# A decoder layer with a mixture of experts: scatters free of one another, another order of score products, more first blocks and more places for blocks

## The chip, the cores and the metric

The kernel runs on one core of one Trainium2 chip. Its five engines appear in the profile as PE (matrix products into PSUM; its weight loads are PEld), DVE (vector work), ACT (activations and copies), POOL (vector work, and here the issue of indirect DMAs, called scatters) and SP (issue of all other DMAs). The metric is device time in microseconds of one execution, lower is better.

## The reference

One decoder layer on 32 sequences of 128 tokens with 128 features: causal self-attention with 16 heads of 8, cross-attention with a second input, and a mixture of 8 experts of which each token uses two; a residual and a layer norm behind each. All in float32.

```python
x = _layernorm(x + _attn(x, x, x, sa_wq, ..., True), ln1_g, ln1_b)
x = _layernorm(x + _attn(x, encoder_output, encoder_output, ca_wq, ..., False), ln2_g, ln2_b)
x = _layernorm(x + _moe(x, router_w, router_b, e_w1, e_b1, e_w2, e_b2), ln3_g, ln3_b)

def _moe(x, rw, rb, w1, b1, w2, b2):
    router_weights = softmax(xf @ rw + rb)
    topw, topi = top_k(router_weights, 2); topw = softmax(topw)
    h = gelu(einsum('td,edf->etf', xf, w1) + b1)        # 128 -> 512
    eo = einsum('etf,efd->etd', h, w2) + b2              # 512 -> 128
    out = sum over the two experts of topw * eo
```

## The kernel before

**The plan.** The kernel states its work as tasks: an engine, an estimated duration, a priority, the tasks it depends on and the buffers it uses. `Plan.run` is a list scheduler. It plays the tasks through with the estimates and the constants `LINK`, `SWITCH`, `PE_LAT` and `CLOCK` at the top of the file, hands out places from pools (`Slots` for SBUF, `Banks` for PSUM), and thereby fixes one order of instructions for each engine. `Plan.emit` writes the instructions in that order and adds what each must wait for: the last instruction of each task it depends on, and the earlier users of its places. For pairs of other engines' instructions it declares that no dependency is to be found by the tensors' addresses (`declare_no_dep`), except on what is kept; for instructions of the same engine it does not. A DMA issued by POOL belongs to POOL's own queue group, so two scatters into one DRAM tensor remain dependent on each other, each on the one ahead.

**Attention.** The 32 sequences are 8 groups of 4 (`NG`, `G`). `prepare` loads a group's input by SP, transposes it on PE (L725), and projects it to q, k (L732, L735) and v (L778). `emit_step` (L835) writes the score products of 59 steps of two halves each. A half computes scores with queries on partitions for the row maxima, taken by DVE (L922), and, three steps later, scores with keys on partitions, to which the negated maxima are added by a product (`sel`) before ACT takes the exponential (L1320); there are 112 halves of each, 14 to a group. All products go through the helper `mm`, L833, which is also used for the products with V. Between the two stands the path of the maxima: POOL splits them into two bfloat16 parts (L934, L935, tile `nmx`), PE transposes them (L942, `nmT`), ACT or DVE copies them out. Norms run on DVE (L1050, L1051) with a power and an affine step on POOL (L1056, L1057, L1147, L1148).

**Routing and rows.** After the cross-attention of a group, `finish_cross` (L1129) computes router scores (L1155), ranks the tokens of each expert with counts on DVE, POOL (L1194 to L1199) and PE (L1206, L1207), and scatters each token's normalised row twice, once per expert, into the DRAM tensor `rows_d`: eight scatters of 128 rows a group (L1227), 64 in all. Eight fill scatters (L1521) complete the last block of each expert.

**Blocks.** `block` (L1544) is called for `NS` = 71 blocks of 128 rows of one expert. SP loads the rows (L1554) and the expert's w1 (L1577, 256 KB); PE transposes the rows (L1565), ACT scales them (L1570), PE does four products with w1 (L1583), ACT four gelus (L1592), PE four products with w2 (L1600), DVE adds b2 (L1610, L1613) and POOL scatters the result into `res_d` (L1618). The first `NF` = 17 blocks use the rows of groups 0 to `GF` = 3 only; the others wait for all rows and the fills. The transposes of all blocks wait for the last attention step (`last_step`). Places are: two of `s_in` for even and four of `s_xT` for odd rows, two of `s_q` for their transposes, three for w1, four for results (`s_o`); a block's PSUM banks come from the four that `kept` leaves to single banks.

**The last norm.** `final` (L1625) loads a group's results (L1632, 512 KB), weights and adds them (L1643, L1646), norms and stores (L1660). It waits for the scatters of a number of blocks, and its tasks stand in the engines' orders between the blocks.

## Time and profile before

| | us |
|---|---|
| median of 3 runs (lowest, highest) | 921.33 (912.32, 924.99) |
| the profiled execution | 923.84 |
| its span, first to last instruction | 922.1 |
| PE, PEld busy | 641.8, 518.2 |
| DVE, ACT, POOL busy | 343.0, 323.2, 259.4 |
| mean granted PE clock | 0.832 |

The views used below: the page gives busy time and the chain of work that ended last, followed backwards; the view of a tile or a line lists its instructions with their durations, and what its engine waited for ahead of them; the waits of an engine sum idle time by what ended it; a timeline lists instructions by start; windows sum busy time in a stretch, with the granted PE clock (1.00 is full) and the DMA engines' mean share and rate. "A <- B" in an instruction reads "A is written from B".

### The profile page before, as it was taken

The numbers are of one execution on the slowest core, as the hardware profiler recorded it, in microseconds if no ns is written. First come the engines' busy times: TensorE is split into PE (matmuls) and PEld (weight loads), VectorE is DVE, ScalarE is ACT, GpSimd is POOL, SyncE is SP. The second block draws the span as 40 slices with busy tenths as digits, with TensorE's granted clock in tenths as the row PEclk, the third lists the DMA queues.
The fourth block names the chain that finished last, engine by engine and source line by source line (L and its number), as shares of the span: only waits on it lengthen the run. The fifth ranks groups of instructions, "written<-read, shape, count | busy, mean of one in ns | idle before, by whom it ended". The sixth has DMA issues, their size and how long they took to land.

```text
span 922.1 us, 31269 instructions
## 1 busy us (share of the span) xinstructions
PE 641.8 (70%) x12884; PEld 518.2 (56%) x12884; DVE 343.0 (37%) x1009; ACT 323.2 (35%) x717; POOL 259.4 (28%) x440
## 2 busy tenths in 40 slices
PE   1888889895986896878957775460776466667760
PEld 1666667673765674657845544450666456567650
DVE  3644445552553453546643514210111431321231
ACT  1233453521632523525313322230244254534430
POOL 4000100213322213231132223423332353423442
PEclk9989999988897997999976857595689798977775
DMA  6200100001001001000002001130344354444321
GB/s 171 83 16 15 38 26 15 27 15 36 26 29 34 14 21 42 19 22 15 5 25 65 17 10 41 44 98 29 84 121 110 112 147 118 127 124 136 105 61 46
DMA packets 53012, 52.73 MB, mean 57 GB/s; under 512 B 7759, under 2 KB 39415, under 8 KB 52872
## 3 DMA queue, kind: packets, MB, share of 16 engines
q1 hardware_dynamic: 44976, 40.74, 15.1%
q0 software_dynamic: 4576, 9.00, 3.0%
q8 instruction: 103, 1.69, 0.8%
q10 hardware_dynamic: 3320, 1.00, 0.5%
q14 instruction: 37, 0.30, 0.1%
HBM read 35.36 MB, written 11.61 MB: 51 GB/s over the span
## 4 chain that ended last, share of the span: by engine, by line
PE 38%; issue 20%; DMA 18%; POOL 10%; DVE 7%; ACT 3%; ACTq 1%; SPq 1%; POOLq 1%; DVEq 0%
PE ps L833 23%; DMA res_d<-o,id 11%; POOL rows_d L1227 6%; DMA rows_d<-y,rid 3%; PE ps L1583 3%; PE ps L1600 2%; DMA pr<-res_d 2%; DVE nm L922 2%; ACT pr L1320 2%; PE ps L778 1%; PE ps L735 1%; PE ps L732 1%; PE ps L1123 1%; PE ps L1155 1%; PE ps L725 1%
## 5 line engine op out<-in xcount | busy, mean ns | idle before, releaser
L922 DVE TENSOR_REDUCE nm<-ps 128x8 f32<-128x1024 f32 (+1 forms) x112 | 136.9, 1224 | 160.5 <-PE ps L833 147.9
L1320 ACT ACTIVATE pr<-ps 128x1024 f32<-128x1024 f32 x112 | 114.7, 1024 | 195.4 <-PE ps L833 182.2
L833 PE MATMUL ps<-k,qm 32*64 32x128 f32 (+1 forms) x4096 | 174.6, 279 | 6.0 <-issue 3.7
L833 PEld LDWEIGHTS ps<-k,qm 32*64 32x64 f32 x4096 | 134.0, 139 | 32.2 <-issue 29.9
L833 PE MATMUL ps<-qm,k 32*64 32x512 f32 (+1 forms) x1024 | 136.6, 609 | 17.5 <-ACT pr L1320 7.0
L1592 ACT ACTIVATE k<-ps,b1c 128x128 f32<-128x128 f32 x284 | 81.1, 372 | 117.6 <-PE ps L1583 75.1
L1583 PE MATMUL ps<-q,w 128*128 128x128 f32 x568 | 97.3, 328 | 33.4 <-DMA w<-in_L_xattn_e_w_dram 22.7
L1618 POOL DMA_INDIRECT res_d<-o,id x71 | 69.9, 985 | 154.0 <-DMA res_d<-o,id 117.2
L1600 PE MATMUL ps<-wall,k 128*128 x568 | 97.1, 325 | 18.4 <-ACT k L1592 11.8
L1583 PEld LDWEIGHTS ps<-q,w 128*128 128x128 f32 x568 | 88.2, 237 | 37.8 <-issue 16.6
L1600 PEld LDWEIGHTS ps<-wall,k 128*128 128x128 f32 x568 | 86.1, 232 | 25.9 <-ACT k L1592 17.8
L1227 POOL DMA_INDIRECT rows_d<-y,rid x64 | 63.8, 997 | 122.5 <-DMA rows_d<-y,rid 109.3
L833 PE MATMUL ps<-pr,v 64*32 64x128 f32 (+2 forms) x3072 | 77.9, 274 | 9.5 <-issue 6.3
L833 PEld LDWEIGHTS ps<-pr,v 64*32 64x32 f32 (+1 forms) x3072 | 60.1, 114 | 22.3 <-issue 12.1
L934 POOL CAST nmx<-nm 128x16 bf16<-128x16 f32 x64 | 12.8, 200 | 198.5 <-DVE nm L922 196.9
L1570 ACT ACTIVATE q<-ps,col_b,col_g 128x128 f32<-128x128 f32 x71 | 33.1, 470 | 75.9 <-PE ps L1565 75.3
L833 PEld LDWEIGHTS ps<-qm,k 32*64 32x64 f32 x1024 | 33.3, 139 | 36.9 <-ACT pr L1320 20.5
L833 PE MATMUL ps<-nmT,sel 32*64 32x128 bf16 x1792 | 51.7, 229 | 2.8 <-issue 2.8
L1610 DVE TENSOR_SCALAR id<-xin,tab_e 128x1 int32<-128x1 f32 x36 | 9.8, 273 | 114.7 <-PE ps L1600 59.0
L942 PE MATMUL ps<-ident,nmx 128*128 128x128 bf16 x64 | 13.4, 240 | 51.4 <-POOL nmx L935 50.2
L833 PEld LDWEIGHTS <-sel 32*64 32x64 bf16 x1792 | 38.2, 111 | 13.2 <-issue 11.8
L1565 PE MATMUL ps<-ident,xT 128*128 128x128 f32 x35 | 11.7, 336 | 45.5 <-DVE o L1613 30.7
(261 smaller groups left out, 857.4 us busy)
## 6 DMA issues: line engine op xcount, KB each, us to landing
w<-in_L_xattn_e_w_dram SPq DMA_DIRECT2D x71, 256.0 KB
qm<-q SPq DMA_DIRECT2D x64, 64.0 KB
pr<-res_d SPq DMA_DIRECT2D x8, 512.0 KB
xin<-rows_d SPq DMA_DIRECT2D x36, 65.0 KB
xT<-rows_d SPq DMA_DIRECT2D x35, 65.0 KB
xin<-in_x_dram SPq DMA_DIRECT2D x8, 256.0 KB
xin<-in_ctx_dram SPq DMA_DIRECT2D x8, 256.0 KB
wall<-in_L_xattn_e_w_dram SPq DMA_DIRECT2D x8, 256.0 KB
```

Source lines behind the costliest of these rows:

```text
L833: nc.tensor.matmul(out_, lhsT=lhsT, rhs=rhs, start=start, stop=stop, skip_group_check=True)
L922: lambda: nc.vector.tensor_reduce(dst(), src(), AX.X, ALU.max, negate=True), [dep], [pair, nm],
L934: nc.gpsimd.tensor_copy(nmx.at[:, a, :, 0:4], src[:, a])
L942: nc.tensor.transpose(b16[:, a * P : (a + 1) * P], nmx.at[:, a].rearrange("p g c -> p (g c)"), ident16)
L1227: nc.gpsimd.indirect_dma_start(out=rows_d[:, :], out_offset=bass.IndirectOffsetOnAxis(ap=rid.at[:, i, k : k + 1], axis=0), in_=y.at[:, i, ...
L1320: lambda kp=kp, prb=prb, kh=kh: nc.scalar.activation(prb.at[:, 8 * kh : 8 * kh + 8, :].rearrange("p h q -> p (h q)"), kp.at.rearrange("p b ...
L1565: nc.tensor.transpose(bt.at[:, 0:P], xr_()[:, 0:P], ident)
L1570: lambda: nc.scalar.activation(xT.at[:, 0:P], bt.at[:, 0:P], AF.Identity, bias=cols["b2"], scale=cols["g2"]),
L1583: nc.tensor.matmul(p1.at[:, c * P : (c + 1) * P], lhsT=w1.at[:, c, :], rhs=xT.at[:, 0:P], start=True, stop=True)
L1592: nc.scalar.activation(h.at[:, c, :], p1.at[:, c * P : (c + 1) * P], AF.Gelu, bias=b1c[:, bass.ds(r + c, 1)],)
L1600: nc.tensor.matmul(p2.at[:, 0:P], lhsT=h.at[:, c, :], rhs=flat[:, bass.ds(w["pe"] + c * P, P)], start=c == 0, stop=c == NFC - 1,)
L1618: nc.gpsimd.indirect_dma_start(out=res_d[:, :], out_offset=bass.IndirectOffsetOnAxis(ap=idb.at[:, 0:1], axis=0), in_=o.at, in_offset=None, ...
```

## The change

- **Scatters.** In `emit`, a task on POOL whose instruction is a DMA is now also declared free of POOL's earlier DMAs, except of those its task or its places name. The eight scatters of a group name none of each other.
- **Order of score products.** `emit_step` collects its pieces (scores with n, masks, `sel` products) with the work time of their row group up to them, and sorts both halves' pieces by it. Cross-attention steps come out as before.
- **Transposes in order.** The transposed input of self-attention is no longer kept as halves interleaved by sequence pair. A projection is one product of 512 columns instead of two of 256; V of self-attention is eight products with 64 rows of result instead of four; the residual in `wo` is one product a sequence instead of two halves.
- **Blocks.** 25 first blocks (`NF`) from groups 0 to 4 (`GF` = 4); blocks take any of eight PSUM banks; rows take any of the six places (`Either`); the transposed rows have three places of their own (`s_bx`); w1 of blocks from 25 on goes into twelve places in the tiles of `qm` (`s_late`).
- **Planner.** `LINK`, `PE_LAT`, `CLOCK` and many durations have new values.

```diff
-LINK = 0.12
+LINK = 0.07
-PE_LAT = 0.1
-CLOCK = 1.08
+PE_LAT = 0.06
+CLOCK = 1.0
...
+class Either(Slots):
+    def take(self, n):
+        for s in self.kinds:
+            if s.free:
+                return s.take(n)
+        return None
...
-        order = [i for i in range(len(self.tiles) - 1, self.kept - 1, -1)]
+        order = list(range(len(self.tiles) - 1, (self.kept if n == 1 else 0) - 1, -1))
...
-                    if key[0] != i.engine:
+                    if key[0] != i.engine or (key[1] and line(i)[1] and t.eng == "POOL"):
                         tc.declare_no_dep(i, group=name, keep=kept, reason="apart, by the plan")
...
-    NF = 17
-    GF = 3
+    NF = 25
+    GF = 4
...
+    s_bx = Slots(places(3, [P, P], "bx"))
...
-        for a in range(2):
-            nc.tensor.matmul(
-                bank[:, 2 * P * a : 2 * P * (a + 1)], lhsT=w,
-                rhs=xT.rearrange("p (a h) (k t) -> p a k h t", a=2, k=2)[:, a], start=True, stop=True,
-            )
+        nc.tensor.matmul(bank, lhsT=w, rhs=xT.rearrange("p s t -> p (s t)"), start=True, stop=True)
...
+                for k in range(2):
+                    nc.tensor.matmul(
+                        bv.at[HALF * k : HALF * k + HALF, i * P : (i + 1) * P],
+                        lhsT=xT.at[:, i - i % 2 + k, HALF * (i % 2) : HALF * (i % 2) + HALF], rhs=raw["wvs"],
+                        start=True, stop=True, skip_group_check=True,
+                    )
...
+            for n in range(len(cols_[0])):
+                nq = cols_[0][n][3]
+                work.append((at, lambda n=n: scores_k(n)))
+                at += 16 * nq * PASS
...
+        for _, fn in sorted(work, key=lambda w: w[0]):
+            fn()
...
-                    for h in range(2):
-                        mm(by.at[HALF * h : HALF * h + HALF, s * P : (s + 1) * P], xs[:, s // 2, s % 2, h], ident, False, False)
+                    nc.tensor.matmul(o, lhsT=it.xT.at[:, s, :], rhs=ident, start=False, stop=False)
...
+    s_xr = Either(s_in, s_xT)
+    s_late = Slots([q_[:, r].rearrange("p (c f) -> p c f", c=NFC) for q_ in qm_t for r in range(4)])
...
-        xr = Buf((s_in, s_xT)[s % 2])
+        xr = Buf(s_xr)
...
-        bt, xT = Buf(s_ps), Buf(s_q)
+        bt, xT = Buf(s_ps, 0), Buf(s_bx)
...
-        p1, p2, h, w1 = Buf(s_ps), Buf(s_ps), Buf(s_k), Buf(s_w1)
+        p1, p2, h, w1 = Buf(s_ps, 0), Buf(s_ps, 0), Buf(s_k), Buf(s_w1 if s < NF else s_late)
```

The line numbers of the kernel after the change are about 40 higher: L1227 becomes L1266, L1618 becomes L1659, L1577 becomes L1618, L934 and L935 become L975 and L976. A name in brackets behind "waits" is a semaphore: that of an engine, or of one of the eight lanes that POOL's DMAs (DMASW) and SP's (DMAHW) take in turn.

The first place is POOL around the scatters of group 0, before:

```order
L934 CAST nmx_164<-nm_161 128x4x4 [waits DVE_49]
L935 TENSOR_TENSOR nmx_164<-nm_161,nmx_164 128x4x4 [waits Pool_49]
L1227 DMA rows_d<-y_185,rid_203 33920x130 [waits DVE_49,Activation_49,DMAHW1_49]
L1227 DMA rows_d<-y_185,rid_203 33920x130 [waits DMASW0_49]
L1227 DMA rows_d<-y_185,rid_203 33920x130 [waits DMASW1_49]
L1227 DMA rows_d<-y_185,rid_203 33920x130 [waits DMASW2_49]
L1227 DMA rows_d<-y_185,rid_203 33920x130 [waits DMASW3_49]
L1227 DMA rows_d<-y_185,rid_203 33920x130 [waits DMASW4_49]
L1227 DMA rows_d<-y_185,rid_203 33920x130 [waits DMASW5_49]
L1227 DMA rows_d<-y_185,rid_203 33920x130 [waits DMASW6_49]
L1056 TENSOR_SCALAR rs_195<-mv_191 128x4 [waits DVE_49]
```

and of the change:

```order
L975 CAST nmx_166<-nm_163 128x4x4 [waits DVE_49]
L976 TENSOR_TENSOR nmx_166<-nm_163,nmx_166 128x4x4 [waits Pool_49]
L1266 DMA rows_d<-y_188,rid_206 33920x130 [waits DVE_49,Activation_49,DMAHW2_49]
L1266 DMA rows_d<-y_188,rid_206 33920x130 x7
L1097 TENSOR_SCALAR rs_198<-mv_194 128x4 [waits DVE_49]
L1098 TENSOR_TENSOR rs_198<-rs_198,mhalf 128x4 [waits Pool_49]
L975 CAST nmx_167<-nm_164 128x4x4 [waits DVE_49]
L976 TENSOR_TENSOR nmx_167<-nm_164,nmx_167 128x4x4 [waits Pool_49]
L1183 COPY y_188<-tok_84 128x4 [waits DMASW4_49,DMASW5_49,DMASW3_49,DMASW6_49,DMASW2_49,DMASW7_49,DMASW1_49,DMASW0_49]
```

Before, each scatter from the second on waits for the lane of the one ahead of it; now the seven behind the first wait for nothing, and the first instruction that waits for all lanes is the reuse of the tile that they read.

The second place is POOL at the end of attention, where group 7's scatters, the fills and the first scatters of block results (to `res_d`) stand, before:

```order
L1618 DMA res_d<-o_256,id_263 8192x128 [waits DVE_49]
L1227 DMA rows_d<-y_186,rid_204 33920x130 [waits DMASW3_49,DMASW2_49,DMASW4_49,DMASW1_49,DMASW5_49,DMASW0_49,DMASW6_49,DVE_49,DMASW7_49,PE_49,Activation_49]
L1227 DMA rows_d<-y_186,rid_204 33920x130 [waits DMASW1_49]
L1227 DMA rows_d<-y_186,rid_204 33920x130 [waits DMASW2_49]
L1227 DMA rows_d<-y_186,rid_204 33920x130 [waits DMASW3_49]
L1227 DMA rows_d<-y_186,rid_204 33920x130 [waits DMASW4_49]
L1227 DMA rows_d<-y_186,rid_204 33920x130 [waits DMASW5_49]
L1227 DMA rows_d<-y_186,rid_204 33920x130 [waits DMASW6_49]
L1227 DMA rows_d<-y_186,rid_204 33920x130 [waits DMASW7_49,DMASW0_49]
L1521 DMA rows_d<-fillrow,fid 33920x130 [waits DVE_49,DMASW0_49]
L1521 DMA rows_d<-fillrow,fid 33920x130 [waits DMASW1_49]
```

and of the change, from the last scatter of group 7 on:

```order
L1266 DMA rows_d<-y_189,rid_207 33920x130 [waits DMASW7_49]
L1560 DMA rows_d<-fillrow,fid 33920x130 [waits DVE_49,DMASW0_49]
L1560 DMA rows_d<-fillrow,fid 33920x130 [waits DMASW1_49]
L1560 DMA rows_d<-fillrow,fid 33920x130 [waits DMASW2_49]
L1560 DMA rows_d<-fillrow,fid 33920x130 [waits DMASW3_49]
L1560 DMA rows_d<-fillrow,fid 33920x130 [waits DMASW4_49]
L1560 DMA rows_d<-fillrow,fid 33920x130 [waits DMASW5_49]
L1560 DMA rows_d<-fillrow,fid 33920x130 [waits DMASW6_49]
L1560 DMA rows_d<-fillrow,fid 33920x130 [waits DMASW7_49]
L1659 DMA res_d<-o_259,id_266 8192x128 [waits DMASW0_49]
L1659 DMA res_d<-o_260,id_267 8192x128 [waits DVE_49,DMASW1_49]
L1659 DMA res_d<-o_261,id_268 8192x128 [waits DVE_49,DMASW2_49]
```

Before, one result's scatter stands ahead of group 7's rows, and each waits for the lane ahead. Now all of group 7's scatters and the fills stand ahead of the first result's, and each waits for its own lane, which is the eighth scatter before it.

The third place is SP at the loads of w1 (into `w`, and now into tiles of `qm`) and of rows (`xin`, `xT`), before:

```order
L1540 TENSOR_LOAD tab_x [waits DMAHW0_49,PE_49]
L1577 ISA
L1577 DMA w_261<-in_L_xattn_e_w_dram 128x512 [waits DMAHW0_49,PE_49]
L1540 TENSOR_LOAD tab_x [waits DMAHW1_49,PE_49]
L1577 ISA
L1577 DMA w_262<-in_L_xattn_e_w_dram 128x512 [waits DMAHW1_49,PE_49]
L1540 TENSOR_LOAD tab_r [waits DMAHW3_49,DVE_49]
L1554 ISA
L1554 DMA xin_137<-rows_d 128x130 [waits DMAHW3_49,DVE_49]
```

and of the change:

```order
L1581 TENSOR_LOAD tab_x [waits DMAHW2_49,PE_49]
L1618 ISA
L1618 DMA w_263<-in_L_xattn_e_w_dram 128x512 [waits DMAHW2_49,PE_49]
L1581 TENSOR_LOAD tab_x [waits DMAHW3_49,PE_49]
L1618 ISA
L1618 DMA w_264<-in_L_xattn_e_w_dram 128x512 [waits DMAHW3_49,PE_49]
L1581 TENSOR_LOAD tab_x [waits DVE_49]
L1618 ISA
L1618 DMA qm_152<-in_L_xattn_e_w_dram 128x512
L1581 TENSOR_LOAD tab_x
L1618 ISA
L1618 DMA qm_152<-in_L_xattn_e_w_dram 128x512 [waits DMAHW4_49]
```

Before, a load of w1 waits for PE to be done with one of the three places; now two in a row do so, and those behind them go to the places in `qm` and wait for no engine.

## Rows read from the trace of the kernel before

**Rows 1.** The page, part 1: busy time, share of span, instructions of each engine.
```profile
PE 641.8 (70%) x12884; PEld 518.2 (56%) x12884; DVE 343.0 (37%) x1009; ACT 323.2 (35%) x717; POOL 259.4 (28%) x440
```

**Rows 2.** The page, part 4: shares of the chain that ended last.
```profile
PE 38%; issue 20%; DMA 18%; POOL 10%; DVE 7%; ACT 3%; ACTq 1%; SPq 1%; POOLq 1%; DVEq 0%
```

**Rows 3.** View of tile rows_d: engine idle before its instructions until (us, times).
```profile
  DMA rows_d<-y,rid: 112.0, 57
```

**Rows 4.** View of tile res_d: duration ns min/median/max, starts; idle before; landing.
```profile
L1618 POOL DMA_INDIRECT res_d<-o,id x71: 967/969/1098, 592.5 to 901.5; - x71
...
  DMA res_d<-o,id: 117.2, 48
...
DMA to landing us min/median/max: 2.1/2.4/5.3
```

**Rows 5.** Timeline of POOL, 204 to 233 us: start, duration, line, operation, [idle before].
```profile
206.99 1.44 POOL L1227 DMA_INDIRECT rows_d<-y,rid  x1 [1.25 <-DVE rc L1020]
...
228.71 0.97 POOL L1227 DMA_INDIRECT rows_d<-y,rid  x1 [1.62 <-DMA rows_d<-y,rid]
...
231.07 0.20 POOL L934 CAST nmx<-nm 128x16 bf16<-128x16 f32 x1
```

**Rows 6.** Waits of PE, 204 to 552 us: us in total, times, longest.
```profile
PE ps L942 <- POOL nmx L935: 50.2, 8, 10.7
```

**Rows 7.** Windows of attention: length, PE PEld DVE ACT POOL busy, PEclk, DMA, GB/s.
```profile
204.00:550.00 346.00, 268.00 (x6797) 203.06 (x6785) 159.13 (x418) 120.28 (x198) 96.73 (x190) 0.85 0.08 25
289.00:337.00 48.00, 43.69 (x1323) 34.43 (x1312) 25.71 (x60) 22.80 (x37) 7.73 (x24) 0.93 0.08 25
```

**Rows 8.** The same windows, exponentials of L1320 alone: length, ACT busy (count).
```profile
204.00:550.00 346.00, 73.76 (x72) 0.85 0.08 25
289.00:337.00 48.00, 13.31 (x13) 0.93 0.08 25
```

**Rows 9.** Timeline 549 to 551 us: the last exponential.
```profile
550.24 1.02 ACT L1320 ACTIVATE pr<-ps 128x1024 f32<-128x1024 f32 x1 [0.76 <-PE ps L833]
```

**Rows 10.** View of line 1613, the block results on DVE: ns, first and last start.
```profile
L1613 DVE TENSOR_TENSOR o<-ps,b2r x71: 280/285/292, 585.1 to 898.2; 128x128 f32<-128x128 f32 x71
```

**Rows 11.** Windows of the blocks, columns as in rows 7.
```profile
620.00:640.00 20.00, 0.00 (x0) 0.00 (x0) 0.00 (x0) 0.00 (x0) 7.71 (x8) 0.56 0.07 24
670.00:680.00 10.00, 8.67 (x67) 7.89 (x67) 1.48 (x6) 5.00 (x17) 2.90 (x3) 1.00 0.46 140
720.00:730.00 10.00, 1.58 (x7) 1.61 (x8) 4.07 (x13) 0.00 (x0) 1.94 (x2) 0.58 0.65 211
```

**Rows 12.** Timeline of PE, 672 to 679 us.
```profile
673.09 1.12 PE L1583 MATMUL ps<-q,w 128*128 128x128 f32 x8
...
674.15 1.06 PE L1600 MATMUL ps<-wall,k 128*128 x8
675.04 1.06 PE L1583 MATMUL ps<-q,w 128*128 128x128 f32 x8
```

**Rows 13.** Waits of PE, 585 to 898 us.
```profile
PE ps L1565 <- DVE o L1613: 41.1, 14, 24.6
PE ps L1583 <- DMA w<-in_L_xattn_e_w_dram: 22.7, 8, 9.1
```

**Rows 14.** Timeline of POOL, 581 to 596 us.
```profile
592.50 1.02 POOL L1618 DMA_INDIRECT res_d<-o,id  x1 [0.55 <-issue]
594.14 0.97 POOL L1227 DMA_INDIRECT rows_d<-y,rid  x1 [0.62 <-DVE fid L1514]
```

**Rows 15.** Timeline of DVE, 206 to 209 us.
```profile
206.90 0.42 DVE L1028 TENSOR_TENSOR u<-u,rc 128x256 f32<-128x256 f32 x1
```

**Rows 16.** Timeline of SP, 498 to 506 us.
```profile
501.14 0.33 SPq L1554 DMA_DIRECT2D xin<-rows_d  x1
501.96 0.33 SPq L1577 DMA_DIRECT2D w<-in_L_xattn_e_w_dram  x1
```

**Rows 17.** Timeline of POOL, 894 to 923 us: the last scatter.
```profile
901.54 0.99 POOL L1618 DMA_INDIRECT res_d<-o,id  x1 [2.17 <-DMA res_d<-o,id]
```

More of the change, by code (lines that the diff above doesn't have):

```diff
@@ L63, with __init__ @@
 class Place:
-    def __init__(self, ap):
-        self.ap, self.last = ap, []
+    def __init__(self, ap, home=None):
+        self.ap, self.last, self.home = ap, [], home
 class Slots:
     def __init__(self, aps):
-        self.free = [Place(ap) for ap in aps]
+        self.free = [Place(ap, self) for ap in aps]
     def take(self, n):
@@ L80, in take, with give, __init__ @@
         return p.ap, [p]
-    def give(self, places):
-        self.free += places
+    def give(self, places, front=False):
+        for p in places:
+            p.home.free.insert(0 if front else len(p.home.free), p)
+class Either(Slots):
+    def __init__(self, *kinds):
+        self.kinds = kinds
+    def take(self, n):
[3 more added lines that the diff above has]
+        return None
 class Banks:
@@ L108, in take, with give @@
         return None
-    def give(self, places):
+    def give(self, places, front=False):
         for i, hs in enumerate(self.halves):
@@ L195, in run @@
                         for b in reversed(taken):
-                            b.slots.give(b.places)
-                            if isinstance(b.slots, Slots):
-                                b.slots.free.insert(0, b.slots.free.pop())
+                            b.slots.give(b.places, True)
                             b.at, b.places = None, []
@@ L713, with transposes @@
     before = {}
-    def transposes(src, prio, deps, bufs, halves=False):
+    def transposes(src, prio, deps, bufs):
         bank = Buf(s_ps)
@@ L751, in prepare @@
         xT = it.xT = Buf(s_xT)
[L752 removed]
+        bank, t = transposes(lambda: it.xin.at, t0 - 6, [ld], [it.xin, xT])
         it.t_tr = t
@@ L837, in emit_step, with rows @@
         kh = 1 - h
+        work = []
+        PASS = 0.427e-3
+        def rows(half, i):
+            rg = 2 * half + i
+            return slice(32 * rg, 32 * rg + 32)
         if sk is not None:
@@ L840, in emit_step, with scores_k @@
             cols_ = sk_cols(sk)
-            for n in range(len(cols_[0])):
+            at = 0.0
+            def scores_k(n):
                 for i in range(2):
-                    rg = 2 * kh + i
-                    rr = slice(32 * rg, 32 * rg + 32)
+                    rr = rows(kh, i)
                     for ct in range(2):
@@ L896, in emit_step, with top_k @@
+            def top_k(r):
+                for i in range(2):
+                    rr = rows(kh, i)
                     for ct in range(2):
@@ L1051, in stats @@
                 nc.vector.bn_aggr(mv.at[:, i, :], st.at[:, i, :])
-            aggr.append(add("DVE", 0.45, prio + 0.01 * i, stats, t_y(i), [*bufs_in, st, mv]))
+            aggr.append(add("DVE", 0.48, prio + 0.01 * i, stats, t_y(i), [*bufs_in, st, mv]))
         def power():
@@ L1184, in part2 @@
             )
-        t2 = add("DVE", 1.4, prio + 1.05, part2, [t1, t_misc], [rt, rti])
+        t2 = add("DVE", 1.05, prio + 1.05, part2, [t1, t_misc], [rt, rti])
         m16 = Buf(s_m16)
@@ L1199, in part3 @@
                 nc.gpsimd.tensor_tensor(dst, c[:, i, :], m[:, i, :], ALU.add)
-        t3 = add("POOL", 1.1, prio + 1.1, part3, [t2, t_cz, cg_done.get(gi - 1)], [rt, m16])
+        t3 = add("POOL", 1.55, prio + 1.1, part3, [t2, t_cz, cg_done.get(gi - 1)], [rt, m16])
         cg_done[gi] = t3
@@ L1594, in gelu @@
                 )
-        t = add("ACT", 1.3, pr0 + 0.5, gelu, [t, t_tab, t_b1c, *exps_all], [p1, h])
+        t = add("ACT", 1.2, pr0 + 0.5, gelu, [t, t_tab, t_b1c, *exps_all], [p1, h])
         def gemm2():
@@ L1613, in result @@
             nc.vector.tensor_tensor(o.at, p2.at[:, 0:P], flat2[:, bass.ds(r, P)], ALU.add)
-        t = add("DVE", 0.6, pr0 + 2, result, [t, t_tab, t_b2r], [p2, xr, o, idb])
+        t = add("DVE", 0.5, pr0 + 2, result, [t, t_tab, t_b2r], [p2, xr, o, idb])
         def scatter():
@@ L1621, in scatter @@
             )
-        t_res.append(add("POOL", 1.2, pr0 + 2.2, scatter, [t], [o, idb], lat=2.2))
+        t_res.append(add("POOL", 1.05, pr0 + 2.2, scatter, [t], [o, idb], lat=2.2))
     def final(gi, s):
```

145 lines of the change are left out of this document (72 added, 73 removed).

## The prediction

> **What bounds the kernel now.** The first view is the busy share of each engine: PE, the matrix engine, is busy 641.8 us of 922.1, 70%, and no other engine passes 37% [rows 1]. The second is the chain of work that ended last: 38% of it is PE, but 18% is DMA, 10% POOL and 20% "issue" [rows 2]. A kernel bound by PE alone would not show a DMA in that chain, so the third view asks which DMA. For the scattered token rows it is the scatter ahead: POOL stood idle for 112.0 us, 57 times, until a scatter to rows_d had landed [rows 3]; for the 71 scatters of block results the same wait is 117.2 us, 48 times, with 0.97 us for one scatter and 2.4 us from issue to landing [rows 4]. So POOL sends a scatter, waits until it lands, and sends the next, though POOL itself is 28% busy.
>
> Does anyone need what POOL holds back? Three stretches answer that, in order of time.
>
> Attention, 204 to 550 us. The eight scatters of group 0 stand in POOL's timeline from 206.99 to 228.71, one each 3.1 us; only behind them comes the split of the score maxima, at 231.07 [rows 5]. PE needs that split for its next transposes and waited for it 8 times, 50.2 us in all, at most 10.7 [rows 6]. In the whole stretch PE was busy 268.00 us of 346 at a mean granted clock of 0.85; from 289 to 337, where no scatter stands, 43.69 of 48 at 0.93 [rows 7]. The exponentials count the work: 72 in 346 us (4.81 us each) against 13 in 48 (3.69) [rows 8]. That the short stretch stands for the whole one can be seen from PE: 268.00/72 = 3.72 us of PE work for one, against 43.69/13 = 3.36, and the quotient 1.11 is nearly that of the clocks, 0.93/0.85 = 1.09.
>
> The change of phase. The last exponential starts at 550.24 [rows 9], the first block result at 585.1, the last at 898.2: 313.1 us for 70 steps between 71 results, 4.47 us a block [rows 10].
>
> The blocks. From 620 to 640 POOL sends the eight fill scatters, one by one, and PE, DVE and ACT do nothing at all; from 670 to 680, undisturbed, PE is busy 8.67 of 10 us at the full clock, ACT 5.00, POOL 2.90; from 720 to 730, behind the first loads for the last norm, PE is down to 1.58 [rows 11]. Back to back a block takes PE 1.95 us, from one first product at 673.09 to the next at 675.04 [rows 12]. What PE waits for longest is a result of DVE, 41.1 us, which is late because its place in SBUF is held by a scatter, and then a w1 load, 22.7 us [rows 13].
>
> **The change, part by part.** *Scatters free.* A scatter keeps its 0.97 us on POOL, but no longer waits for the one ahead. The order shows no wait among the eight of a group; later scatters wait for the eighth before them, and results for the place of the fourth before them. At 0.97 us each, four take 3.9 us, more than the 2.4 of a landing, so I cost these waits at nothing. That POOL can issue before a landing is seen once: 592.50 (res_d) and 594.14 (rows_d), 1.64 us apart, less than the shortest landing of 2.1 [rows 4, 14].
>
> A scatter can be slower than 0.97: the first of group 0 took 1.44 [rows 5] while DVE ran an operation with two SBUF inputs beside it [rows 15]. The Trainium skill, page "SBUF — State Buffer", section "SBUF: two separate sides", has a rule that speaks against the change here: POOL and such a DVE operation share a port pair as an exclusive lock, and a scatter's descriptors are written by POOL. By that rule eight scatters at 1.44 would hold POOL 11.5 us instead of 7.8 per group; the row agrees once, and no row shows it eight times.
>
> Term 1, attention. Eight scatters now hold POOL some 8 us where 24 us passed from first scatter to split (206.99 to 231.07). The old hold of 24 cost PE at most 10.7 us [rows 6], so about 13 us of it were covered, and 8 (or 11.5) fits in that. So the stretch runs at the pace of the undisturbed one: 72 × 3.69 = 266, **80 us less**. The lower bound is the direct wait alone, 50.2 us; the upper is PE without any idle time, 72 × 3.36 = 242, 104 less.
>
> Term 2, change of phase. The 34.9 us from the last exponential to the first result hold the last groups' norms and routing, which stay. What is new stands on POOL: in the order all eight scatters of group 7 and the eight fills come ahead of the first result's scatter, where one result went first before. That is 16 × 0.97 = 15.5 us during which four places take results; four blocks at the pace below are 10 us. Since group 7's routing on POOL also starts earlier, because group 6's eight scatters pass in 8 us, I take **7 us more** (0 to 15.5).
>
> Term 3, the blocks. With scatters at 0.97 us, 25 first blocks that need no fill (25 × 2.54 = 64 us of work while the last rows and fills land), eight banks instead of four, six row places and twelve w1 places, every wait of [rows 13] loses its cause and PE sets the pace. From 670 to 680 it did 67 matmul records, of which a block has 17 (8, 8 and a transpose): 10 × 17/67 = 2.54 us [rows 11]. I take that: 70 × 2.54 = 178, **135 us less**. The lower bound is 1.95, another 41 less. The upper is the loads: 256 KB of w1, 65 of rows and 64 of scatter are 385 KB a block; at the 140 GB/s of 670 to 680 that is 2.75 us (15 us more), at the 211 GB/s of 720 to 730, 1.82 [rows 11]. SP issues a load each 0.82 us, 1.64 for a block's two [rows 16], ACT's 5.00 of 10 us [rows 11] leave half: neither bounds.
>
> Term 4, the end. The last result's scatter waited 2.17 us for the one ahead [rows 17]; with its own 0.99 in the shadow of the next, **3 us less**. The rest of the tail, the last load, norm and store, is a chain and stays.
>
> *At nothing.* V of self-attention as eight products instead of four per group is 4 more; a product is two records of 0.14 us [rows 12], so 4 × 0.28 = 1.1 us a group, 9 in all. The residual in one product instead of two halves saves the same 9; projections do the same columns in one instead of two. The new order of score products leaves their number, and the cross-attention steps, as they were; PE's idle time in the undisturbed stretch is 4.31 us for 13 exponentials, 0.33 each, so it can give back at most 24 us of the stretch (inside the upper bound of term 1), and I let it cost as much at worst. The planner's new constants only move work in time. In the first 204 us no scatter stands, and I leave it.
>
> Sum, against the profiled execution (923.84; 1.74 lie outside its span of 922.1): 923.84 − 80 + 7 − 135 − 3 = 713. The median of the three runs shown, 921.33, lies 2.5 below that execution, so **710 us**. Its own range: attention −24 to +30, phase −7 to +8.5, blocks −41 to +15; these are unlikely to add up on one side, so 660 to 745.
>
> **Rivals.** *B: the blocks turn from scatters to loads and norms.* The loads for the last norm (512 KB each) stand in SP's queue between the blocks' loads, and the norms on DVE between the results; for that PE fell to 1.58 us of 10 [rows 11], 8 us lost. Eight such groups lose 8 × 8 = 64: 710 + 64 = about 774, a pace of 3.45. For it: the same order of queues after the change, three loads in a row. Against: the w1 places let SP run 12 blocks ahead.
>
> *C: only the direct wait goes in attention.* 50 instead of 80: 740. For it: PE's clock, 0.85 over the stretch, could stay low. Against: it was 0.93 wherever PE was not held.
>
> *D: scatters still go one after another,* because POOL's queue completes each before it takes the next, so that the change doesn't do what it says. Then attention stays, the first results too, and from 592.50 on 16 + 71 scatters at 3.1 us are 270 us, to 862; with the 22.3 us from the last scatter's start to the end, 884, less 2.5: about 882. Against it stands the pair of [rows 14], to two tensors. The Trainium skill, page "DMA: Bandwidth & Descriptors", section "SWDGE vs HWDGE vs iDMA", states that one queue and context is allocated for such transfers, which would point to D; but the same row shows one queue taking a second scatter before the first could land.
>
> *E: slower.* Up to eight scatters in flight crowd out the loads of rows and w1 on the same DMA engines. It decides when a block takes (921 − 710)/70 = 3.0 us longer than 2.54, 5.5 us; 930 at 5.7. Against: the wait for w1 was 22.7 us over 71 blocks, 0.3 each [rows 13], and would have to grow tenfold, while 211 GB/s went through at need [rows 11].
>
> **How the numbers follow.** The likeliest 0.66 (710), B 0.18 (774), C 0.08 (740), D 0.05 (882), E 0.03 (930). The range leaves out D, E, the upper end of B and a little under 660: 660 to 785. A measurement of this kernel tells about 2% from no change, 903 to 940. Faster by more: all of the first three and most of D, 0.96; within 2%: the rest of D and a part of E, 0.02; slower 0.02.
>
> **What would show it.** In the profile after: scatters of a group about 1 us apart on POOL, and no wait for rows_d or res_d ahead of them; PE's wait for the split under 10 us in all; the last exponential near 470 us and the first result near 505; POOL's first res_d scatter after 16 others; results 2.5 us apart with PE over 8 of 10 us and a granted clock near 1.0, and no 20 us hole at the fills; the end some 20 us behind the last result. It is wrong in term 1 if PE waits in attention for something else at once, in term 3 if results stay over 3 us apart, and altogether if scatters still stand 3 us apart.

## The result and the profile after

The changed kernel takes **743.95 us** (median of 4 runs, 737.44 to 744.84) against 919.75 of the kernel before on the same occasions: the ratio is 0.808, 95% interval 0.800 to 0.815. The forecast was 710 with a range of 660 to 785. The profiled execution after took 744.84 us with a span of 743.1, so that it stands 179.0 us below the 923.84 of before, where the sum had 211.

The page after, busy time and the chain of work that ended last (the lines that answer to [rows 1, 2]):

```profile
PE 588.1 (79%) x12852; PEld 475.0 (64%) x12852; DVE 341.3 (46%) x1009; ACT 321.0 (43%) x717; POOL 259.5 (35%) x440
...
PE 62%; issue 10%; ACT 7%; DMA 7%; DVE 6%; POOL 3%; SPq 2%; ACTq 2%; DVEq 1%; POOLq 0%
```

PE is now 62% of the chain instead of 38, DMA 7 instead of 18, POOL 3 instead of 10. PE itself is busy 54 us less with all but the same products, since its clock is higher (0.893 in the mean, 0.832 before).

The view of tile rows_d after (what POOL waited for ahead of its instructions on that tile), against [rows 3]:

```profile
L1266 POOL DMA_INDIRECT rows_d<-y,rid x64: 971/972/1260, 204.7 to 523.8; - x64
...
  issue: 19.4, 63
```

The 112.0 us behind the scatter ahead are gone; what is left is "issue", 63 times 0.3 us. POOL's timeline after, from the last scatters of group 7's rows to the first of a block's result, shows what one scatter costs now:

```profile
514.79 1.03 POOL L1266 DMA_INDIRECT rows_d<-y,rid  x1 [1.44 <-ACT k L1633]
516.12 0.97 POOL L1266 DMA_INDIRECT rows_d<-y,rid  x1 [0.30 <-issue]
...
525.06 0.97 POOL L1560 DMA_INDIRECT rows_d<-fillrow,fid  x1 [0.30 <-issue]
...
535.27 0.97 POOL L1659 DMA_INDIRECT res_d<-o,id  x1 [0.30 <-issue]
...
722.23 1.00 POOL L1659 DMA_INDIRECT res_d<-o,id  x1 [0.15 <-issue]
```

Sixteen scatters took 535.27 − 514.79 = 20.5 us, 1.28 each and not 0.97: between two there are 0.30 us in which POOL waits for nothing that the profile shows.

Windows of attention after, exponentials of line 1359 alone (length, ACT busy with count, granted clock, DMA share, GB/s), against [rows 8]:

```profile
213.10:421.40 208.30, 57.30 (x56) 0.96 0.08 25
421.40:485.95 64.55, 16.19 (x16) 0.79 0.14 41
```

56 exponentials took 3.72 us each, and the last 16 4.0 at a clock of 0.79. What PE waited for from 204 to 486 us, against [rows 6]:

```profile
PE ps L845 <- issue: 7.5, 9, 1.7
PE ps L734 <- ACT y L1111: 7.0, 1, 7.0
```

The split of the maxima, 50.2 us before, is no longer among the waits. One wait of 7.0 us is new in its weight: the last group's self-attention norm, with no other group left to cover it.

The result line after, against [rows 10], and windows of the blocks with the results of line 1654 alone:

```profile
L1654 DVE TENSOR_TENSOR o<-ps,b2r x71: 279/284/293, 512.0 to 717.3; 128x128 f32<-128x128 f32 x71
```

```profile
560.00:600.00 40.00, 5.13 (x18) 1.00 0.57 158
609.20:717.70 108.50, 10.04 (x36) 0.89 0.48 142
```

70 steps take 205.3 us, 2.93 each: 2.2 where nothing is in the way (18 results in 40 us, clock 1.00), 3.1 from 609 us on, where the last norms stand between the blocks. And there is one hole, in PE's timeline:

```profile
528.70 1.16 PE L1641 MATMUL ps<-wall,k 128*128 x8 [0.77 <-ACT k L1633]
543.68 0.45 PE L1606 MATMUL ps<-ident,xT 128*128 128x128 f32 x1 [13.82 <-DMA xT<-rows_d]
544.74 2.08 PE L1624 MATMUL ps<-bx,w 128*128 128x128 f32 x8 [0.61 <-DVE o L1654]
```

PE waits 13.82 us for a load of rows, and its next products take 2.08 us instead of the 1.06 of full clock (the granted clock is 0.50 from 543.6 to 553.0 us).

| | before | after | forecast |
|---|---|---|---|
| last exponential starts | 550.2 | 484.9 | 470 |
| first result | 585.1 | 512.0 | 505 |
| last result | 898.2 | 717.3 | 690 |
| end of the profiled execution | 923.84 | 744.84 | 713 |

### The profile page after: what moved, and what is told of

Its sections match the earlier page's. It is cut to its first block, busy times and chain, and to the rows that moved or that the text cites. A ratio compares the mean times of both kernels' runs of the same rounds, so it can differ in the third digit from the quotient of the medians.

```text
span 743.1 us, 31241 instructions
## 1 busy us (share of the span) xinstructions
PE 588.1 (79%) x12852; PEld 475.0 (64%) x12852; DVE 341.3 (46%) x1009; ACT 321.0 (43%) x717; POOL 259.5 (35%) x440
## 4 chain that ended last, share of the span: by engine, by line
PE 62%; issue 10%; ACT 7%; DMA 7%; DVE 6%; POOL 3%; SPq 2%; ACTq 2%; DVEq 1%; POOLq 0%
PE ps L845 35%; PE ps L1624 6%; PE ps L1641 6%; PE ps L740 4%; ACT pr L1359 3%; DVE nm L963 2%; PE ps L1606 2%; ACT k L1633 2%; DMA xT<-rows_d 1%; ACT y L1111 1%; POOL rows_d L1266 1%; PE ps L734 1%; PE ps L781 1%; PE ps L1132 1%; DMA res_d<-o,id 1%
## 5 line engine op out<-in xcount | busy, mean ns | idle before, releaser
L845 PE MATMUL ps<-qm,k 32*64 32x512 f32 (+1 forms) x1024 | 131.7, 590 | 16.2 <-ACT pr L1359 5.4
L975 POOL CAST nmx<-nm 128x16 bf16<-128x16 f32 x64 | 12.9, 201 | 249.2 <-DVE nm L963 242.5
L1641 PE MATMUL ps<-wall,k 128*128 x568 | 82.5, 292 | 17.1 <-ACT k L1633 13.3
L1659 POOL DMA_INDIRECT res_d<-o,id x71 | 69.8, 983 | 60.0 <-DVE o L1654 47.7
L845 PE MATMUL ps<-pr,v 64*32 64x64 f32 (+2 forms) x3072 | 76.0, 271 | 14.2 <-issue 10.1
L1641 PEld LDWEIGHTS ps<-wall,k 128*128 128x128 f32 x568 | 72.3, 200 | 22.0 <-ACT k L1633 15.1
L1266 POOL DMA_INDIRECT rows_d<-y,rid x64 | 64.2, 1003 | 28.9 <-issue 17.3
L1624 PE MATMUL ps<-bx,qm 128*128 128x128 f32 x368 | 55.5, 301 | 0.0
L1651 DVE TENSOR_SCALAR id<-xT,tab_e 128x1 int32<-128x1 f32 x47 | 12.8, 273 | 89.3 <-PE ps L1606 21.9
L1624 PEld LDWEIGHTS ps<-bx,qm 128*128 128x128 f32 x368 | 51.3, 216 | 0.4 <-ACT bx L1611 0.3
L1611 ACT ACTIVATE bx<-ps,col_b,col_g 128x128 f32<-128x128 f32 x71 | 32.3, 468 | 30.8 <-PE ps L1606 30.5
L1606 PE MATMUL ps<-ident,xT 128*128 128x128 f32 x47 | 15.0, 319 | 24.2 <-DMA xT<-rows_d 18.6
L1111 ACT ACTIVATE y<-ps,rs 128x128 f32<-128x128 f32 x64 | 24.7, 460 | 16.9 <-DVE rs L1103 16.9
## 6 DMA issues: line engine op xcount, KB each, us to landing
pr<-res_d SPq DMA_DIRECT2D x8, 512.0 KB
```

Source lines behind the costliest of these rows:

```text
L845: nc.tensor.matmul(out_, lhsT=lhsT, rhs=rhs, start=start, stop=stop, skip_group_check=True)
L1111: lambda i=i: nc.scalar.activation(dst(i), src(i), AF.Identity, bias=rs.at[:, 1, i : i + 1], scale=rs.at[:, 0, i : i + 1],),
L1266: nc.gpsimd.indirect_dma_start(out=rows_d[:, :], out_offset=bass.IndirectOffsetOnAxis(ap=rid.at[:, i, k : k + 1], axis=0), in_=y.at[:, i, ...
L1606: nc.tensor.transpose(bt.at[:, 0:P], xr_()[:, 0:P], ident)
L1611: lambda: nc.scalar.activation(xT.at[:, 0:P], bt.at[:, 0:P], AF.Identity, bias=cols["b2"], scale=cols["g2"]),
L1624: nc.tensor.matmul(p1.at[:, c * P : (c + 1) * P], lhsT=w1.at[:, c, :], rhs=xT.at[:, 0:P], start=True, stop=True)
```

## The experiments

Two questions: which part of the change carries the 176 us, and where the 32 us are that the sum promised and the chip did not give.

**Scatters free, alone, and everything else, alone.** The line of the change that frees the scatters, put into the kernel before, and taken out of the kernel after:

```diff
# kernel before, e1_before_free
-                    if key[0] != i.engine:
+                    if key[0] != i.engine or (key[1] and line(i)[1] and t.eng == "POOL"):
# kernel after, e2_after_serial
-                    if key[0] != i.engine or (key[1] and line(i)[1] and t.eng == "POOL"):
+                    if key[0] != i.engine:
```

> The kernel before with the one line of the change that frees POOL's scatters of one another; its order of instructions, its 17 first blocks and its places stay. Theory (the free scatters carry most of the gain): scatters of a group 1.27 us apart as in the changed kernel, last exponential near 485 us, no 20 us hole at the fills, blocks at 3 to 3.5 us, the last of the places and orders missing: 770 to 800 us in all. Rival (the gain needs the new order and the places as well): 840 us or more.

> The changed kernel with that one line taken back, so that each scatter waits for the one ahead; everything else is new. Theory: scatters 3.1 us apart, last exponential back at 540 to 550 us, 16 + 71 scatters one by one behind it: 860 to 900 us. Rival (new order, places and first blocks carry the gain): under 800 us.

Measured: 772.29 us with the free scatters alone (ratio 0.839, 0.834 to 0.843) and 908.80 with everything else alone (0.988, 0.984 to 0.991), against 919.64 of the kernel before on the same chip. (The changed kernel did not run beside e1 to e4; their traces show the same course as its own in the second and third set of scatters, where PE does 229 and 264 products in e3_after_12_results and 224 and 263 in the changed kernel. Why that has to be looked at is said in the last section.) So of the 176 us the scatters alone give 147 and the rest alone 11; the rest is worth 28 once scatters are free. What was expected of the second was 860 to 900: the direction held, but the bound by scatters is harder than I thought. The view of tile res_d of e2_after_serial says why:

```profile
L1659 POOL DMA_INDIRECT res_d<-o,id x71: 964/969/1102, 633.8 to 887.3; - x71
...
  DMA res_d<-o,id: 111.3, 49
```

71 scatters in 253.5 us, 3.6 each and not 3.1, with waits for the last norms' work between them. In the free one the exponentials and results lie at:

```profile
L1320 ACT ACTIVATE pr<-ps x112: 1018/1023/1026, 53.2 to 477.5; 128x1024 f32<-128x1024 f32 x112
```

```profile
L1613 DVE TENSOR_TENSOR o<-ps,b2r x71: 279/285/293, 511.0 to 748.5; 128x128 f32<-128x128 f32 x71
```

The last exponential at 477.5 is even 7 us ahead of the changed kernel's 484.9, so that in attention as a whole the other edits give nothing; its blocks take 237.5 us instead of 205.3. The 28 us of the rest are the blocks (32 less), with 4 lost behind the last result.

**The hole at 530 us.** Eight more places for block results, cut out of the tiles of q:

```diff
+    q_t = places(2, [P, G * P], "q")
+    s_q = Slots(q_t)
...
-    s_o = Slots(places(4, [P, P], "o"))
+    s_o = Slots(places(4, [P, P], "o") + [q_[:, r * P : (r + 1) * P] for q_ in q_t for r in range(4)])
...
-    s_id = Slots(places(4, [P, 1], "id", I32))
+    s_id = Slots(places(12, [P, 1], "id", I32))
```

> The changed kernel with twelve places for block results instead of four (the eight new ones lie in the two tiles of q, idle by then). Theory: the 13.8 us hole of PE at 530 us is block results without a place behind 16 scatters, whose rows then hold their places too; with twelve places it closes, and with it the low clock behind it: 13 to 17 us less, 727 to 731 us, results 5 to 12 before the first scatter of a result. Rival (rows of a later group or a load are what is late): the hole stays, within 4 us of 744.

Measured: 729.98 us (725.90 to 731.29), 14 below the changed kernel, as expected. In DVE's timeline of that kernel the results go on while POOL is at its fills (fifth to eleventh result, into places of q):

```profile
517.07 0.28 DVE L1655 TENSOR_TENSOR q<-ps,b2r 128x128 f32<-128x128 f32 x1
...
529.88 0.28 DVE L1655 TENSOR_TENSOR q<-ps,b2r 128x128 f32<-128x128 f32 x1
537.89 0.28 DVE L1655 TENSOR_TENSOR q<-ps,b2r 128x128 f32<-128x128 f32 x1
```

In the changed kernel nothing came between the fourth result (517.5) and the fifth (540.1). Its row numbers (`id`, which also have four places) waited for the landing of a result's scatter:

```profile
539.95 0.27 DVE L1651 TENSOR_SCALAR id<-xT,tab_e 128x1 int32<-128x1 f32 x1 [17.31 <-DMA res_d<-o,id]
```

So the load of rows that PE waited for was only the last link: 16 scatters hold POOL, the fifth result has no place, its rows keep theirs, and the next load can't start. In the profiled executions (744.84 and 729.52) the blocks take 194.8 us instead of 205.3; the first result came 4.4 us earlier as well, which this edit can't have done, so the places are worth 10 to 14 us.

**The late blocks.** All last norms behind the last block, by having each wait for it:

```diff
-        final(gi, (done if gi >= GF else NF + max(E, done - NF)) - 1)
+        final(gi, NS - 1)
```

> The changed kernel with all eight last norms behind the last block, instead of between the blocks. Theory: from 609 us on it is the norms in DVE's order that hold the results up (3.1 us a block instead of 2.19 before); without them all blocks from 560 us run at 2.2 us, and the last result comes near 685 us instead of 717; the eight norms then make the end longer, 50 to 60 us instead of 26 from the last result, 735 to 750 in all. Rival (loads of w1 into the late places, or six row places, limit the late blocks): pace stays near 3 us, last result later than 705 us, 760 or more in all.

Windows of that kernel, results alone, and the line of the results:

```profile
560.00:600.00 40.00, 5.13 (x18) 1.00 0.57 163
605.50:683.00 77.50, 10.08 (x36) 1.00 0.47 131
```

```profile
L1654 DVE TENSOR_TENSOR o<-ps,b2r x71: 280/284/292, 509.2 to 682.5; 128x128 f32<-128x128 f32 x71
```

The late blocks run at 2.2 us and a full clock, and the last result comes at 682.5: the pace theory holds, neither w1 loads nor row places are in the way. In all it is slower, 766.38 us (764.35 to 768.75), and here the expectation was wrong: eight norms one behind another need 86 us behind the last result, not 50 to 60.

**First blocks, places, order of products, norms spread.** Four edits of the changed kernel: `NF` and `GF` back to 17 and 3; the blocks' old banks and places; the old order of pieces in a step; and, on top of the twelve result places, each sequence's sum of a last norm tied to a later result.

```diff
# e5_after_17_first
-    NF = 25
-    GF = 4
+    NF = 17
+    GF = 3
# e6_after_old_places
-        xr = Buf(s_xr)
+        xr = Buf((s_in, s_xT)[s % 2])
...
-        bt, xT = Buf(s_ps, 0), Buf(s_bx)
+        bt, xT = Buf(s_ps), Buf(s_q)
...
-        p1, p2, h, w1 = Buf(s_ps, 0), Buf(s_ps, 0), Buf(s_k), Buf(s_w1 if s < NF else s_late)
+        p1, p2, h, w1 = Buf(s_ps), Buf(s_ps), Buf(s_k), Buf(s_w1)
# e7_after_old_products
-                work.append((at, lambda n=n: scores_k(n)))
+                work.append((0, lambda n=n: scores_k(n)))
...
-                    work.append((at + 0.001, lambda r=r, n=n: scores_q(r, n)))
+                    work.append((1, lambda r=r, n=n: scores_q(r, n)))
# e8_norms_spread
+        t_out.append(t)
...
-                add("DVE", 2 * 0.345, pr0 + 0.2 + 0.01 * i, sums, [t, items["c", gi].t_w, items["c", gi].t_x2], [r, y])
+                add("DVE", 2 * 0.345, pr0 + 0.2 + 0.01 * i, sums,
+                    [t, items["c", gi].t_w, items["c", gi].t_x2, t_out[min(s + 5 + i, NS - 1)]], [r, y])
...
-        final(gi, (done if gi >= GF else NF + max(E, done - NF)) - 1)
+        final(gi, (done if gi >= GF else NF + max(E, done - NF) + 3 * gi) - 1)
```

(In the third, masks with queries, masks with keys and maxima come under 2, 3 and 4.)

> The changed kernel with 17 first blocks from groups 0 to 3 again, instead of 25 from 0 to 4. Theory: with free scatters the last fill lands near 537 us, when only four to ten results are out, so the 18th block never waits for it; the count of first blocks is worth nothing now: 738 to 750 us. Rival (first blocks cover the fills, as the sum assumed): PE idle for another 10 us or more near 545 us, 755 us or more.

> The changed kernel with the blocks' old places: four PSUM banks, rows in even and odd places by turns, two places of q for their transposes, three places of w1. Theory (places carry the pace of the blocks once scatters are free): between 560 and 600 us a result each 2.8 to 3.3 us instead of 2.19, 760 to 780 in all. Rival (PE or the norms carry it): pace within 0.2 us of 2.2 there, under 750.

> The changed kernel with the old order of pieces in a step of score products (scores with keys first, then all with queries, masks, maxima last). Theory: the new order is what brought exponentials 40 to 96 to 3.72 us each, against 3.91 in the kernel before with free scatters alone; with the old order they take about 3.9, 8 to 14 us more in all, 752 to 758. Rival (the planner's durations and transposes in order do it, the order of products nothing): 3.72 stays, 740 to 748.

> The changed kernel with twelve places for results, and each sequence's sum of the last norm put on DVE behind a later block's result: the first not before the fifth result after the block that the norm waits for, one result between two sums, and the norms of groups 1 to 3 three blocks later than one another. Theory: late blocks lose their pace to norms that hold DVE (and results behind them) while their load has not landed; now they run at 2.2 to 2.5 us, the last result near 685 us, 705 to 716 in all. Rival (their loads crowd out those of the blocks, whatever DVE's order): late blocks stay at 2.8 us or more, 722 or more.

Measured: 824.47, 875.90, 820.87 and 796.11 us, with the kernel before at 915.38 beside them. None of the totals is near what any theory gave, and all are longer; that is followed up below. What can be read inside one run still counts. The old places against the new ones, in an undisturbed stretch of e6_after_old_places and of e8_norms_spread (16 results in either, of which 15 steps):

```profile
655.60:699.20 43.60, 4.40 (x16) 1.00 0.49 137
```

```profile
637.50:670.70 33.20, 4.26 (x16) 1.00 0.58 160
```

2.9 us a block with the old places, 2.2 with the new ones, both at full clock: the places carry the pace, as expected. (e8 has twelve result places too; the changed kernel, with four, shows the same 2.2 from 560 to 600 us.) The three others were run again with the changed kernel beside them.

> The changed kernel itself, so that the three kernels beside it have their own yardstick on the same chip: in the four runs before this one all of attention took 50 to 60 us more than in the first runs, whatever had been edited, with a granted clock of 0.84 where it had been 1.00. Theory (that is the chip's clock under a denser PE, not the edits): 744 us if the clock from 205 to 265 us is near 1.0, some 800 to 820 if it is near 0.85. Rival (the edits cost it): 744 us at either clock.

> The changed kernel with the old order of score products, beside the changed kernel on one chip. Theory (the order of products brought the steady pace of attention): 8 to 14 us above e9_after_again. Rival (it does nothing, the planner's durations do): within 4 us of it.

> The changed kernel with twelve places for results and the last norms spread over DVE's order. Theory: 14 us (places) and another 14 to 22 us (late blocks at 2.2 to 2.5 us instead of 3.1) below e9_after_again, 28 to 36 us in all. Rival (their loads crowd out the blocks'): 16 us or less below it.

> The changed kernel with 17 first blocks instead of 25, beside the changed kernel on one chip. Theory: the fills land before the 18th block is reached, so the count is worth nothing: within 6 us of e9_after_again. Rival (first blocks cover the fills): 11 us or more above it.

Measured, on another chip than the four before: 744.13 us for the changed kernel (ratio 0.805, 0.800 to 0.811), 746.99 with the old products (0.809, 0.803 to 0.815), 721.49 with the norms spread (0.782, 0.777 to 0.787), 737.04 with 17 first blocks (0.798, 0.793 to 0.803).

- The changed kernel took 744 us at a granted clock of 1.00 from 205 to 265 us, as the theory said; e8_norms_spread had 0.84 there. The same three files took 74 to 87 us less here. The totals of e5 to e8 are not their edits' doing; they belong to that chip, or to that visit to it (last section).
- Old order of products: 3 us, inside the intervals. The exponentials from 213 to 421 us, first of e9_after_again and then of e10_old_products_again, are 56 in both:

```profile
213.00:421.00 208.00, 56.43 (x56) 0.96 0.08 25
```

```profile
213.00:421.00 208.00, 57.31 (x56) 0.96 0.08 26
```

  So my theory on the order of products falls. In e1_before_free, where all other edits are missing, 56 took 219 us:

```profile
208.40:427.40 219.00, 57.31 (x56) 0.95 0.09 29
```

  What makes 3.72 us of these 3.91 is one of the planner's values, the places or the transposes in order; I have not told these apart, and since the last 16 exponentials are slower after the change than in e1, nothing of it reaches the end of attention.
- 17 first blocks: 7 us faster than 25, not slower, and 1 us outside the 6 that the theory allowed. That more first blocks cover nothing holds. Some 3 of the 7 lie in attention, whose last exponential starts at 479.4 us instead of 482.7 (term 1 below shows the wait that is missing there); why the rest is better stays open.
- Norms spread: 22.6 below the changed kernel, the fastest kernel here. By the totals 14 of them are the result places (e3), so that the spread itself is worth 8 to 9, where 14 to 22 were expected. The late blocks' window in e11_norms_spread_again:

```profile
596.40:696.70 100.30, 9.96 (x36) 0.93 0.51 154
```

  36 results in 100.3 us are still 2.9 each. With the places alone (e3) the last 36 took 104.4, and in the changed kernel 108.5 and, in e9_after_again, 112.6; as one kernel differs by 4 us, it isn't shown that DVE's order made the late blocks faster. Some 23 us against the 77.5 of e4 remain with the norms among the blocks, and whether it is their loads of 512 KB or the work itself is open.

## Why the prediction was right, and where it missed

**The bound.** Right: the kernel was bound by scatters that waited for each other, through PE's wait for the split in attention, the fills and the results. e1 and e2 show it: 147 us by that line alone.

**A scatter at 0.97 us, its waits at nothing.** The waits are nothing (1.0 us in all for res_d), the cost is 1.28: the 0.30 us between two scatters is a term that the sum lacked, and that [rows 5] could not show, where each gap held a landing. The feared 1.44 for each didn't come: 53 of the 64 scatters took 0.97 to 1.00 us. A set's first scatter takes 1.03 to 1.23, also where DVE runs nothing beside it (1.12 at 499.28), so most of that length is not DVE's doing. Three others took 1.17 to 1.26, each beside DVE's L1069, an operation with two SBUF inputs; the clearest began while DVE still had 0.3 us to run:

```profile
212.52 0.42 DVE L1069 TENSOR_TENSOR u<-u,rc 128x256 f32<-128x256 f32 x1
...
212.62 1.17 POOL L1266 DMA_INDIRECT rows_d<-y,rid  x1 [0.30 <-issue]
```

That agrees with what the Trainium skill, page "SBUF — State Buffer", section "SBUF: two separate sides", says of the lock: the one who starts first holds the pair. (For a DVE operation with two SBUF inputs the section names only POOL operations that read SBUF, a condition that the prediction left out; the inputs of the scatter are y and rid.) Here it costs 0.2 to 0.3 us now and then.

**Term 1, attention.** 80 forecast, 65.3 measured (550.2 to 484.9). The step that failed is "72 × 3.69 from 204 us". The pace was right where groups overlap, 3.72. But the first of the 72 starts at 213.1, not 3.7 us behind 204 (5.4 us), the 56 are 0.03 slower each (1.7), and the last 15 steps take 4.23 (8.1): together the 15 us that are missing.

The 5.4 us lie in the part that the prediction left alone, ahead of 204 us: the very first exponential already starts at 60.0 us instead of 54.8. With the same code of attention it starts at 54.6 in e2_after_serial and at 60.5 in e6_after_old_places, so what moves it is not shown.

The 8.1 us are mostly one wait of PE, and its cause is a set of scatters. The fifth set stands on POOL from 428.55 to 438.82; the norm's statistics that DVE finished at 431.68 wait behind it for POOL's step L1097, and PE for the norm:

```profile
431.50 0.18 DVE L1092 BATCH_NORM_AGGREGATE mv<-st 128x2 f32<-128x6 f32 x1
...
437.84 0.97 POOL L1266 DMA_INDIRECT rows_d<-y,rid  x1 [0.30 <-issue]
...
438.84 0.26 POOL L1097 TENSOR_SCALAR rs<-mv 128x4 f32<-128x4 f32 x1
...
442.01 1.11 PE L734 MATMUL ps<-ident,y 128*128 128x128 f32 x4 [6.97 <-ACT y L1111]
```

So what failed there is "about 13 us of it were covered, and 8 fits in that": a set holds POOL for 10.3 us, and with the last group's norm next PE had little else to do. Windows of the fifth set (length, PE PEld DVE ACT POOL busy with counts, clock, DMA share, GB/s), first of the changed kernel, then of e12_17_first_again:

```profile
428.55:438.82 10.27, 4.76 (x65) 4.05 (x62) 5.73 (x24) 0.00 (x0) 8.13 (x8) 0.94 0.14 45
```

```profile
423.95:434.05 10.10, 9.78 (x256) 8.17 (x239) 8.04 (x18) 3.07 (x3) 7.95 (x9) 1.00 0.16 49
```

In e12 there are 256 products beside the same set; at L734 PE then waits 1.5 us at most, and the last 15 steps take 3.4 each. With the scatters one by one (e2_after_serial) the same wait is 16.1 us. The end of attention need not be slow: in e1_before_free, with the order of before, its last 15 steps take 3.3.

**Term 2, change of phase.** From the last exponential to the first result 27.1 us instead of 34.9, which I had let stand. The scatters don't explain that: with them alone free it is 33.5 (e1, 477.5 to 511.0), and with everything else alone 28.6 (e2, 544.5 to 573.1), so other edits shorten it, and which is not known. The stall that I put at 7, with 15.5 as the upper bound, is the 10 to 14 of e3. That the two together make 3 to 6 us more, near the 7 forecast, is luck. The mechanism was named (16 scatters ahead of the first result's, four places); mis-sized were the scatter (1.28) and the cover, four results' worth of blocks, since a result without a place also holds its rows' place.

**Term 3, the blocks.** 128 us less forecast with the stall of term 2, 107.8 measured (313.1 to 205.3). The undisturbed pace of 2.54 was too slow: 2.2. It was lost again: 36 late results at 3.1 us, where 2.2 gives 31 us less. That is rival B, which I priced at 64 for eight groups of norms: half of it came, beside the forecast and not instead of it. e4 shows it as the norms' doing, and acquits the loads of w1.

**Term 4, the end.** Not seen: 27.5 us from the last result to the end instead of 25.6. POOL's last scatter no longer waits for the one ahead (0.15 us), but it stands behind a norm's two steps on POOL and three scatters of results that came in a burst.

**At nothing.** The order of products: shown (e10). First blocks: shown to be no gain (e12). Products of V, the residual and the projections were not tried alone.

**The rivals.** D (scatters still one by one) is out: scatters start 1.28 us apart. C (50 us in attention) is half out: the 65.3 lie midway between its 50 and the 80 of the sum, and the low clock that it needs was gone in the middle (0.96) and stayed for the last 16 exponentials (0.79). That a page of the Trainium skill, "DMA: Bandwidth & Descriptors", section "SWDGE vs HWDGE vs iDMA", speaks of one queue and context did not mean one scatter at a time. E, slower by crowding, is out.

The 32 us between the sum (713) and the profiled execution (744.84) are 15 in attention, 20 in the blocks with their stall and 5 behind the last result, less 8 from the last exponential to the first result.

## What to carry to other kernels

Find out first whether queued DMAs wait for each other because of the hardware or because a scheduler sees one tensor: here a single declaration gave 147 of 176 us, and new order and places were worth 11 without it and 28 with it. When a wait is removed, price the burst that it had spread out (16 scatters at 1.28 us against four result places), and ask what stands behind each burst in its engine's order: a norm's step of 0.26 us behind eight scatters cost PE 7.0 us. Before two kernels are compared, run both on the same chip: here the same file differed by 10 to 12% from one chip to another.

## What the runs showed of the hardware that was not expected

On the chip of e5 to e8, eight scatters in a row nearly stop PE, and with it the others. The windows of the second and third set of group scatters, all engines (length, PE PEld DVE ACT POOL busy with counts, clock, DMA share, GB/s), first of e8_norms_spread, then of e11_norms_spread_again, the same file on another chip:

```profile
255.05:265.19 10.14, 6.66 (x94) 2.97 (x87) 1.96 (x6) 0.04 (x1) 7.98 (x8) 0.71 0.14 48
324.68:334.77 10.09, 6.37 (x72) 2.43 (x63) 0.24 (x3) 0.05 (x1) 7.95 (x9) 0.65 0.14 46
```

```profile
247.76:258.18 10.42, 10.26 (x224) 8.41 (x223) 7.34 (x15) 3.22 (x5) 8.29 (x9) 0.91 0.15 48
310.02:320.12 10.10, 9.33 (x266) 7.20 (x265) 7.75 (x16) 4.19 (x6) 7.96 (x9) 1.00 0.25 76
```

POOL does the same in both, 8.0 us for eight scatters. PE issues 94 and 72 products instead of 224 and 266, DVE 6 and 3 operations instead of 15 and 16, ACT one instead of 5 and 6. PE's timeline in e8_norms_spread shows how:

```profile
261.43 0.37 PE L846 MATMUL ps<-maskq,idj 32*64 32x256 bf16 x1 [0.27 <-issue]
262.14 0.41 PE L846 MATMUL ps<-nmT,sel 32*64 32x128 bf16 x5 [0.34 <-issue]
263.58 0.33 PE L846 MATMUL ps<-nmT,sel 32*64 32x128 bf16 x3 [1.02 <-issue]
```

A few products come each 0.7 or 1.4 us, with "issue" between them: no semaphore is late, the instructions are. DVE and ACT are not shown to be held in the same way: in the first window their next instructions wait 9.82 and 11.74 us for PE, in the second the trace names no instruction that released them.

The sets of scatters are where the two runs part. The first and the last exponential of a row between the first and the second set, in e8_norms_spread and then in e11_norms_spread_again:

```profile
219.47 1.02 ACT L1360 ACTIVATE pr<-ps 128x1024 f32<-128x1024 f32 x1 [1.85 <-PE ps L846]
...
243.73 1.02 ACT L1360 ACTIVATE pr<-ps 128x1024 f32<-128x1024 f32 x1 [1.63 <-PE ps L846]
```

```profile
212.05 1.02 ACT L1360 ACTIVATE pr<-ps 128x1024 f32<-128x1024 f32 x1 [1.85 <-PE ps L846]
...
236.31 1.02 ACT L1360 ACTIVATE pr<-ps 128x1024 f32<-128x1024 f32 x1 [1.63 <-PE ps L846]
```

The row lies 7.42 us apart at both its ends. The next row of this kind, behind two more sets, lies 25.24 us apart at its start (343.97 and 318.73) and 25.53 at its end (371.89 and 346.36). Away from the scatters the program thus runs nearly alike on both chips, and two sets add 17.8 us. By the last result the distance is 73.8 us (770.1 and 696.3). So it is around the scatters that the changed kernels lose their 74 to 87 us, while the kernel before, whose scatters stand 3 us apart, took 915.38 there and 921.95 on the chip of e9 to e12. What holds the instructions back isn't in the trace. Each chip was visited once, so that chip and occasion can't be told apart, the changed kernel itself wasn't run on that chip, and that a burst does it is read from the place in time, not tried by spacing the scatters.
